# A bias that enters a PSUM bank by a three-row matmul instead of a ScalarE copy, and sums moved between two products (graph convolution, one Trainium2 core)

## The chip, the core and the metric

The kernel runs on one core of one Trainium2 chip. Its engines each run their own list of instructions in order and wait for each other by semaphores: PE (TensorE, matrix products into PSUM; its weight loads are shown apart as PEld), DVE (VectorE), ACT (ScalarE), POOL (GpSimd, which here issues scatters) and SP (SyncE, which issues the other transfers). The metric is the device time of one execution in microseconds.

## The reference

A graph layer over 12,500 nodes with 128 features and 412,500 edges, sorted by destination:

```python
h = jnp.maximum(_layernorm(x, axis=-1), 0.0)        # 12500 x 128
hh = h @ W_in2f
Wij = ssp(f_ij @ W_f1 + b_f1) @ W_f2 + b_f2         # per edge; f_ij is 412500 x 20, ssp = softplus - log 2
Wij = Wij * rcut_ij[:, None]
x_ij = hh[idx_j] * Wij                              # idx_j = dst
agg = segment_sum(x_ij, idx_i)                      # idx_i = src
out = x + ssp(agg @ W_o1 + b_o1) @ W_o2 + b_o2
```

The change concerns `b_f2`, which is added to the second product of every edge.

## The kernel before

Edges are worked off in chunks of 512 (four tiles of 128), four chunks to a group. There are 836 chunks: 660 plain ones, and 176 of the groups listed in SORTED ("permuted" groups), whose edges are first brought into another order on the core (class Permute: prefix counts and products with one-hot matrices, in "ready", "product", "taken" and "moved" phases spread over the steps ahead). No scatter of a permuted chunk starts after 3750 us.

A chunk passes through these stages:

- `hidden`: z = f @ W_f1 for two chunks at once (PE); `hidden_exp` and `hidden_log` make the softplus r from it (ACT).
- `window` and `pick`: a one-hot matrix `at` selects the rows of h for each edge out of a narrow table, four products into a PSUM bank called picked (PE).
- `picked`: hg = picked times the edge's weight, four ACT instructions.
- `bias` and `value`: a PSUM bank v is filled with b_f2, by an ACT copy (for the first two chunks by a product with a row of ones), and r @ W_f2 is accumulated on it, four float32 products on PE that don't clear the bank.
- `message`: o = v * hg (DVE).
- `put`: one indirect DMA per tile writes o to slots in DRAM (POOL): four scatters in a plain chunk. In a permuted chunk only the first tile is scattered, and the other three go out by a static transfer of SP.
- `blocks`, `rank`, `rank_end`: each edge's slot is a running count per node block; PE accumulates counts in the bank free, DVE reads their maximum (top).

The edges are cut into six segments (SEGS). When a segment has been scattered, class Collect reads its slots back (`load`, SP, into m), compares (`compare`, DVE, into to) and sums them per node (`add`, PE, into the bank acc); `keep` adds a finished bank to agg (ACT for the first segment, DVE later). The first such sums run after 1300 us; those of the last segment follow after the loop.

Everything is put in order by hand: `step(k)` issues, for each engine, the pieces of several chunks. Before the change PE's order within a step is value of chunk k+1, picking of chunk k+2, products of the permuting, hidden, rank, and the sums of the step's slots. ACT's is exponent, copies of permuted data, hg of chunk k+1, copy of b_f2 for chunk k+2, logarithm. The banks of picked and v share one pool of three. PACE makes the first scatter of chunk k wait for the picking of chunk k+2.

The banks that the change touches are v (filled at L969, products at L976) and picked (L985); hg is L994 and L1121, the message L1005 and L1131, the scatters L1014 and L1137, the sums L1430, keep L1451 and L1453, the exponent L871, the logarithm L876, the copy out of z L1330.

Of the kernel before, what the change touches and what calls it, by code (L numbers as in the profile page):

```python
# [69 lines left out]
def gnn_kernel(  # L70
# [142 lines left out]
    def sbuf(name, shape, dtype=F32):  # L213
        return const.tile(shape, dtype, name=name)

    def spread(t, n):
        return t[:, None, :].to_broadcast([t.shape[0], n, P])
# [20 lines left out]
    bf1, bo1 = (sbuf(n, [P, 1]) for n in ("bf1", "bo1"))  # L238
    bf2, bo2 = (sbuf(n, [P, P]) for n in ("bf2", "bo2"))
    nbo1 = sbuf("nbo1", [P, 1])  # L240
    spare = sbuf("spare", [P, 1])
    prow = sbuf("prow", [WP, 1])
    ones = sbuf("ones", [P, 1])
# [162 lines left out]
    def clear_sums():  # L406

        nc.vector.memset(exps, 0.0)

    def permute_constants():  # L410

# [286 lines left out]
    with tc.tile_pool(name="edge", bufs=2) as edge, tc.tile_pool(  # L698
# [65 lines left out]
        class Group:  # L764
# [194 lines left out]

            def bias(self, c):  # L960


                v = psum.tile([P, QT, P], F32, name="v", bufs=3)
                if self.g * NCHUNK + c < 2:
                    nc.tensor.matmul(v.rearrange("p t f -> p (t f)"),
                                     ones[0:1, :].to_broadcast([1, P]), spread(bf2[0:1, :], QT),
                                     start=True, stop=False, skip_group_check=True)
                else:
                    nc.scalar.activation(v, spread(bf2, QT), AF.Copy)  # L969
                return v  # L970

            def value(self, c, v):

                r = self.pair[c // 2 * 2][:, c % 2, :]
                for i in range(QT):
                    done = nc.tensor.matmul(v[:, i, :], r[:, i * P:(i + 1) * P], wf2,  # L976
                                     start=False, stop=True, skip_group_check=True)
                behind_of["value", place_of[self.g, c]] = done.ins.name
                return v
# [479 lines left out]
        def of(k):  # L1459
            return groups[steps[k][0]], steps[k][1]  # L1460

        hgs, ats, vs, bs = {}, {}, {}, {}

        compared = []
        owed = []
# [47 lines left out]
        def step(k, units=(), aside=()):  # L1513

            def has(j):
                return 0 <= j < NCH

            group(steps[max(0, min(k + LG, NCH - 1))][0])  # L1520
            part("rows", min(k + LW, 2 * k + 3, NEXT if k < NEXT - 3 else NCH), rows)
            for out_, in_ in statics:
                nc.sync.dma_start(out_, in_)
            statics.clear()
            if not aside:
                sorting(k, "taken")
            part("exp", min(k + LZ - 1, made["hidden"]), pairs(hidden_exp))
            if has(k):
                g, c = of(k)
                g.message(c, vs.pop(k), hgs.pop(k))  # L1530
            sorting(k, "moved")
            if aside:
                sorting(k, "taken")
            for m in aside:
                next(m, None)
            if k == place_of[permuted[-1], 0]:
                all_moved()
            if has(k + 1):
                g, c = of(k + 1)
                hgs[k + 1] = g.picked(c, ps.pop(k + 1))  # L1540
                vs[k + 1] = g.value(c, bs.pop(k + 1))
            if has(k + 2):
                g, c = of(k + 2)
                ps[k + 2] = psum.tile([P, QT, P], F32, name="picked", tag="v", bufs=3)
                g.pick(c, ats.pop(k + 2), ps[k + 2])
                if k + 2 > 0:
                    bs[k + 2] = g.bias(c)
            part("blocks", min(k + LR + 1, 2 * k + 3), blocks)
            for c, u in units:
                c.compare(u)  # L1550
                compared.append((c, u))
            if has(k):
                g, c = of(k)
                g.put(c)
            sorting(k, "product")
            part("hidden", k + LZ, pairs(hidden))
            for m in aside:
                next(m, None)
            part("log", min(k + LZ - 2, made["exp"]), pairs(hidden_log))
            for r in tops:  # L1560
                for _ in r:
                    pass
            tops.clear()
            upto = max(made["rank"], min(k + LR, 2 * k + 3))
            ready = [ranks(j) for j in range(made["rank"] + 1, upto + 1)]
            made["rank"] = upto
            for r in ready[:-1]:
                for _ in r:
                    pass
            for r in ready[-1:]:  # L1570
                next(r, None)
                tops.append(r)
            for c in owed:
                c.keep()
            owed.clear()
            part("window", k + 3, window)
            for c, u in units:
                c.load(u + AHEAD)
            for c, u in compared:
                c.add(u)  # L1580
            compared.clear()
            sorting(k, "ready")

        zeros = {}
# [143 lines left out]
        with tc.manual_schedule():  # L1728
# [22 lines left out]
            next(h[0])  # L1751
            part("rows", 1, rows)
            clear_sums()
            bs[0] = groups[0].bias(0)
            group(1)
            aside = side()
            prepares = permute_constants()
# [173 lines left out]
```

## Time and profile before

| | |
|---|---|
| median of 3 runs | 4806.63 us (4789.95 to 4812.86) |
| profiled execution | 4812.01 us, span 4809.8 us |
| mean granted PE clock | 0.855 |
| ACT copies of b_f2 (L969) | 834, 605 ns each |
| value products (L976) | 6688 records (two for each float32 product), 304 ns mean |
| scatters (L1014, L1137) | 2640 and 176, 964 and 962 ns |
| sums of slots (L1430) | 8492 records, 305 ns mean |

A row of the grouped views has the line, engine, operation, tiles written and read, count; then the busy time in us, the mean ns of one, the idle time of the engine just ahead of these instructions and what ended most of it. Matmuls overlap, so the busy time of a group is less than count times mean. In a timeline row stand start, duration, engine, line, operation, and in brackets the idle time before it with what ended it. "issue" means that the profile shows nothing that was waited for, "remote" that the one who ended the wait isn't told.

### The profile page before, as it was taken

The page shows a single profiled execution, that of the slowest core. Times are in us where ns is not written, and L with a number is a line of the kernel's source. Part 1 is how long each engine was busy: PE and PEld are TensorE (multiplying, and loading weights), DVE is VectorE, ACT ScalarE, POOL GpSimd, SP SyncE. Part 2 cuts the span into 40 slices and gives each one's busy share as a digit, 9 for nine tenths or more (in the row PEclk, how much of TensorE's full clock was granted, in tenths as well). Part 3 has the DMA queues.
Part 4 walks back from the last instruction along what each step waited for, and adds up shares of the span by engine and source line. Part 5 has one row for each costly group of instructions (what it writes and reads, how often), then busy time and mean ns, then how long its engine had stood idle before and what let it go on. Part 6 is the DMA issues. An engine that isn't in the chain of part 4 may idle for free. (4 is left out here: it accounts for less than half of the span.)

```text
span 4809.8 us, 81802 instructions
## 1 busy us (share of the span) xinstructions
PE 3657.9 (76%) x24283; PEld 2818.2 (59%) x24356; DVE 3165.3 (66%) x8788; ACT 2541.9 (53%) x5816; POOL 2716.4 (56%) x2834
## 2 busy tenths in 40 slices
PE   6666676666667777777877778888777878888878
PEld 4444444444446556665656666666666666676767
DVE  6667666655556666666666666767756666666667
ACT  4566566655655555555555555555544444444434
POOL 4655556555655555555555555555556666666650
PEclk8777778777778898888888888889989999889999
DMA  5676555544546655556655556667667787666666
GB/s 155 188 254 209 146 166 171 170 135 122 140 138 197 169 167 163 150 163 207 198 143 147 148 161 170 174 195 215 189 179 204 203 233 213 183 184 189 186 176 193
DMA packets 745252, 853.19 MB, mean 177 GB/s; under 512 B 288269, under 2 KB 546077, under 8 KB 744801
## 3 DMA queue, kind: packets, MB, share of 16 engines
q1 hardware_dynamic: 654256, 661.57, 50.8%
q0 software_dynamic: 90112, 186.17, 11.6%
q8 instruction: 198, 3.24, 0.3%
q14 instruction: 254, 2.07, 0.1%
q10 hardware_dynamic: 432, 0.13, 0.0%
HBM read 427.59 MB, written 402.53 MB: 173 GB/s over the span
## 5 line engine op out<-in xcount | busy, mean ns | idle before, releaser
L1014 POOL DMA_INDIRECT slots<-o,slot x2640 | 2544.3, 964 | 1625.3 <-issue 650.6
L1430 PE MATMUL acc<-to,m 128*128 128x128 f32 (+1 forms) x8492 | 1241.2, 305 | 194.3 <-issue 116.1
L1430 PEld LDWEIGHTS acc<-to,m 128*128 128x128 f32 (+1 forms) x8492 | 1186.4, 218 | 329.5 <-issue 190.0
L976 PE MATMUL v<-wf,r 128*128 128x128 f32 x6688 | 1041.7, 304 | 128.5 <-issue 76.4
L976 PEld LDWEIGHTS v<-wf,r 128*128 128x128 f32 x6688 | 961.4, 218 | 229.9 <-issue 145.2
L871 ACT ACTIVATE r<-z,bf 128x1024 f32<-128x1024 f32 x418 | 464.6, 1111 | 1085.7 <-remote 387.7
L994 ACT ACTIVATE hg<-picked,rcut 128x128 f32<-128x128 f32 x2640 | 748.2, 369 | 510.5 <-PE acc L1430 181.6
L1005 DVE TENSOR_TENSOR o<-v,hg 128x512 f32<-128x512 f32 x660 | 453.2, 687 | 672.9 <-remote 221.4
L1414 DVE TENSOR_TENSOR to<-count_ps,m 128x640 f32<-128x640 f16 (+6 forms) x988 | 678.0, 721 | 102.4 <-ACT scalars L1343 38.3
L969 ACT ACTIVATE v<-bf 128x512 f32<-128x512 f32 x834 | 504.9, 605 | 114.4 <-DVE o L1005 40.2
L911 DVE TENSOR_REDUCE top<-free 128x4 f32<-128x392 f32 x660 | 368.0, 558 | 213.0 <-remote 87.0
L985 PE MATMUL picked<-near,at 96*128 96x128 bf16 x2640 | 283.6, 234 | 264.9 <-issue 84.2
L876 ACT ACTIVATE r<-r,half 128x1024 f32<-128x1024 f32 x418 | 476.2, 1139 | 0.0
L863 PE MATMUL z<-f,wf 20*128 20x512 f32 x1320 | 430.7, 728 | 9.2 <-issue 5.1
L937 PE MATMUL free<-inb,rest_of 128*128 128x392 f16 x704 | 258.2, 367 | 227.4 <-DVE top L911 119.7
L985 PEld LDWEIGHTS <-at 96*128 96x128 bf16 x2640 | 223.2, 106 | 312.4 <-issue 260.8
L880 DVE TENSOR_TENSOR inb<-count_ps,blk 128x392 f16<-128x392 f16 x660 | 365.3, 554 | 1.5 <-PE acc_p L1264 1.5
L1137 POOL DMA_INDIRECT slots<-o,slot_p x176 | 169.3, 962 | 325.6 <-PE picked L985 150.5
L1121 ACT ACTIVATE hg<-picked,scalars 128x128 f32<-128x128 f32 x704 | 199.5, 370 | 129.9 <-remote 67.5
L906 PE MATMUL free<-inb,after 128*128 128x392 f16 x660 | 244.0, 370 | 18.6 <-DVE used L943 9.5
L1330 ACT ACTIVATE xo<-z 128x1024 bf16<-128x1024 f32 x88 | 90.0, 1023 | 272.5 <-PE z L1325 122.7
L956 DVE TENSOR_SCALAR at<-rel,prow 96x512 bf16<-96x512 bf16 x660 | 233.1, 353 | 0.0
(228 smaller groups left out, 3113.4 us busy)
## 6 DMA issues: line engine op xcount, KB each, us to landing
m<-slots SPq DMA_DIRECT2D x360, 322.5 KB
m<-slots SPq DMA_DIRECT2D x222, 387.0 KB
rel<-rel_d SPq DMA_DIRECT2D x165, 384.0 KB
slots<-zero SPq DMA_DIRECT2D x98, 516.0 KB
slots<-o,slot POOLq DMA_INDIRECT x2640
fix<-o SPq DMA_DIRECT2D x176, 193.5 KB
f<-in_f_n SPq DMA_DIRECT2D x416, 80.0 KB
m<-slots SPq DMA_DIRECT2D x90, 258.0 KB
```

The costliest lines, as they stand in the source:

```text
L863: nc.tensor.matmul(z[:, k, :], wf1[rows, :], self.f[rows, :], start=True, stop=True)
L871: nc.scalar.activation(r, z, AF.Exp, bias=bf1, accum_out=exps[:, i:i + 1])
L876: nc.scalar.activation(r, r, AF.Ln, bias=half, scale=0.5)
L911: nc.vector.tensor_reduce(self.top[:, c * QT:(c + 1) * QT], free_v, axis=mybir.AxisListType.X, op=ALU.max)
L969: nc.scalar.activation(v, spread(bf2, QT), AF.Copy)
L976: done = nc.tensor.matmul(v[:, i, :], r[:, i * P:(i + 1) * P], wf2, start=False, stop=True, skip_group_check=True)
L985: done = nc.tensor.matmul(ps[:, i, :], at[:, i * P:(i + 1) * P], near, start=i == 0, stop=i == QT - 1, skip_group_check=True)
L994: nc.scalar.activation(hg[:, i, :], ps[:, i, :], AF.Copy, scale=self.rcut[:, j:j + 1])
L1005: nc.vector.tensor_mul(o[:, :, :P], v, hg)
L1014: put = nc.gpsimd.indirect_dma_start(out=views[next(turns) % VIEWS], out_offset=bass.IndirectOffsetOnAxis(ap=self.slot[:, j:j + 1], axis=0 ...
L1414: nc.vector.tensor_tensor(to[:p, a:e, :], count_ps[:p, None, :].to_broadcast([p, e - a, P]), self.m[u][:p, a:e, P:].to_broadcast([p, e - a ...
L1430: nc.tensor.matmul(self.acc[b // self.size][:, i, :], m[:p, j, :P], to[:p, j, :], start=t == 0, stop=t == self.seg.read(b) - 1)
```

## The change

b_f2 is split once, at the start, into three bfloat16 rows whose sum is the float32 row (six DVE instructions in `clear_sums`). For all chunks but the first two, v is then started by one product of three rows of ones with these three rows, in place of the ACT copy. The bank is taken just ahead of the value products and no longer a step earlier. Four things move in `step(k)`: hg and value of chunk k+1 go to the head of the step, ahead of the exponent and of the message; the slots that were compared in the step before are summed between value and picking (they were summed at the end of their own step); keep, unmoved, now follows in the same step as the sums; and the logarithm goes ahead of the side work that prepares the tables.

```diff
+    ones3, bf2_parts = (sbuf(n, [P, P], BF16) for n in ("ones3", "bf2_parts"))
...
     def clear_sums():
         nc.vector.memset(exps, 0.0)
+        nc.vector.memset(ones3, 1.0)
+        w = ln.tile([P, P], F32, name="w_left", bufs=1)
+        def high(a):
+            return a.bitcast(BF16).rearrange("p (f h) -> p f h", h=2)[:, :, 1]
+        nc.vector.tensor_scalar(bf2_parts, high(bf2), ident[:, 0:1], None, op0=ALU.mult)
+        nc.vector.tensor_sub(w, bf2, high(bf2))
+        nc.vector.scalar_tensor_tensor(bf2_parts, high(w), ident[:, 1:2], bf2_parts,
+                                       op0=ALU.mult, op1=ALU.add)
+        nc.vector.tensor_sub(w, w, high(w))
+        nc.vector.scalar_tensor_tensor(bf2_parts, high(w), ident[:, 2:3], bf2_parts,
+                                       op0=ALU.mult, op1=ALU.add)
...
             def bias(self, c):
...
                 else:
-                    nc.scalar.activation(v, spread(bf2, QT), AF.Copy)
+                    nc.tensor.matmul(v.rearrange("p t f -> p (t f)"), ones3[:3, :],
+                                     spread(bf2_parts[:3, :], QT),
+                                     start=True, stop=False, skip_group_check=True)
                 return v
-            def value(self, c, v):
+            def value(self, c):
+                v = self.bias(c)
...
         def step(k, units=(), aside=()):
...
             statics.clear()
+            if has(k + 1):
+                g, c = of(k + 1)
+                hgs[k + 1] = g.picked(c, ps.pop(k + 1))
+                vs[k + 1] = g.value(c)
             if not aside:
                 sorting(k, "taken")
             part("exp", min(k + LZ - 1, made["hidden"]), pairs(hidden_exp))
...
-            if has(k + 1):
-                g, c = of(k + 1)
-                hgs[k + 1] = g.picked(c, ps.pop(k + 1))
-                vs[k + 1] = g.value(c, bs.pop(k + 1))
+            for c, u in compared:
+                c.add(u)
+            compared.clear()
             if has(k + 2):
...
                 g.pick(c, ats.pop(k + 2), ps[k + 2])
-                if k + 2 > 0:
-                    bs[k + 2] = g.bias(c)
...
             part("hidden", k + LZ, pairs(hidden))
+            part("log", min(k + LZ - 2, made["exp"]), pairs(hidden_log))
             for m in aside:
                 next(m, None)
-            part("log", min(k + LZ - 2, made["exp"]), pairs(hidden_log))
...
                 c.load(u + AHEAD)
-            for c, u in compared:
-                c.add(u)
-            compared.clear()
             sorting(k, "ready")
...
-            bs[0] = groups[0].bias(0)
```

The instructions of SP and POOL keep their order, and DVE's too but for the six at the start. On PE, around the value products of chunk 720 (a plain one; wf_63 is W_f2, after is a constant of the ranking, `[waits ...]` names the engines and DMA queues that an instruction waits for), there stood:

```order
L906 LDWEIGHTS after
L906 MATMUL free<-inb,after 128x392
L1430 MATMUL acc<-to,m 128x128 [waits DMAHW7_49]
L1430 MATMUL acc<-to,m 128x128 x4
L1430 MATMUL acc<-to,m 128x128 [waits DMAHW2_49]
L1430 MATMUL acc<-to,m 128x128 [waits DMAHW3_49]
L1430 MATMUL acc<-to,m 128x128 x3
L976 MATMUL v<-wf_63,r 128x128 [waits PE_49,Activation_49]
L976 MATMUL v<-wf_63,r 128x128 x3
L985 LDWEIGHTS at [waits DVE_49]
L985 MATMUL picked<-near,at 128x128 [waits DVE_49]
```

The sums stood ahead of the value products; these waited for ACT (the copy of b_f2), and the picking for DVE (the message, whose bank it takes). In the same place now:

```order
L982 LDWEIGHTS ones_71
L982 MATMUL v<-bf_parts,ones_71 128x512
L992 MATMUL v<-wf_63,r 128x128 [waits Activation_49]
L992 MATMUL v<-wf_63,r 128x128 x3
L1446 MATMUL acc<-to,m 128x128 [waits DMAHW7_49]
L1446 MATMUL acc<-to,m 128x128 x4
L1446 MATMUL acc<-to,m 128x128 [waits DMAHW2_49]
L1446 MATMUL acc<-to,m 128x128 [waits DMAHW3_49]
L1446 MATMUL acc<-to,m 128x128 x3
L1001 LDWEIGHTS at [waits DVE_49]
L1001 MATMUL picked<-near,at 128x128 [waits Activation_49]
```

The bias product and the value products stand ahead of the sums, and the picking's first row waits for ACT (hg of the chunk before). On ACT, in a stretch with permuted chunks (scalars are a permuted chunk's weights, xo takes its permuted features out of z), before:

```order
L876 ACTIVATE r<-r,half 128x1024
L871 ACTIVATE r,exps<-z,bf_66 128x1024
L1121 ACTIVATE hg<-picked,scalars 128x128 x4
L969 ACTIVATE v<-bf_68 128x512
L1330 ACTIVATE xo<-z 128x1024
L1121 ACTIVATE hg<-picked,scalars 128x128 x4
L969 ACTIVATE v<-bf_68 128x512
L876 ACTIVATE r<-r,half 128x1024
```

and now:

```order
L890 ACTIVATE r<-r,half 128x1024
L1137 ACTIVATE hg<-picked,scalars 128x128 x4
L885 ACTIVATE r,exps<-z,bf_66 128x1024
L1137 ACTIVATE hg<-picked,scalars 128x128 x4
L1346 ACTIVATE xo<-z 128x1024
L890 ACTIVATE r<-r,half 128x1024
```

hg has moved ahead of the exponent and of the copy out of z, and the copies of b_f2 are gone.

More of the change, by code (lines that the diff above doesn't have):

```diff
@@ L1460, in of @@
             return groups[steps[k][0]], steps[k][1]
-        hgs, ats, vs, bs = {}, {}, {}, {}
+        hgs, ats, vs = {}, {}, {}
         compared = []
```

## The prediction

> **What bounds the kernel now.** I read the page first (shares by engine, costliest groups), then busy time by stage, then the waits of POOL, then two pieces of the timeline.
>
> ```profile
> span 4809.8 us, 81802 instructions
> ...
> PE 3657.9 (76%) x24283; PEld 2818.2 (59%) x24356; DVE 3165.3 (66%) x8788; ACT 2541.9 (53%) x5816; POOL 2716.4 (56%) x2834
> ...
> L1014 POOL DMA_INDIRECT slots<-o,slot x2640 | 2544.3, 964 | 1625.3 <-issue 650.6
> ...
> L969 ACT ACTIVATE v<-bf 128x512 f32<-128x512 f32 x834 | 504.9, 605 | 114.4 <-DVE o L1005 40.2
> ```
>
> No engine is full. PE is the busiest at 76%, and the work to be removed is 505 us of ScalarE, which has room. POOL's share of 56% misleads: its 2640 scatters show 964 ns each, but most follow each other after another 0.3 us that is not counted as busy (650.6 us over the 2080 waits put down to issue). So a chunk's four scatters hold POOL for about 4 x 1.27 = 5.1 us. By stage:
>
> ```profile
> 3750.00:4640.00 890.00, 732.33 (x5275) 619.17 (x5275) 571.34 (x1233) 405.00 (x938) 552.68 (x577) 0.91 0.70 197
> 2500.00:3650.00 1150.00, 918.50 (x6396) 738.13 (x6419) 778.76 (x2086) 600.65 (x1382) 642.32 (x668) 0.88 0.63 175
> ...
> 130.00:1300.00 1170.00, 785.84 (x4520) 520.87 (x4539) 753.19 (x2496) 704.41 (x1633) 682.85 (x704) 0.78 0.59 170
> ```
>
> The columns are the stretch, its length, busy time and count of PE, PEld, DVE, ACT and POOL, the granted clock, DMA share and GB/s. In the last stretch there are only plain chunks: 577 scatters are 144.25 steps, 890/144.25 = 6.17 us a step, of which PE is busy 732.33/144.25 = 5.08 us. What sets 6.17? The timeline there:
>
> ```profile
> 4261.27 0.96 POOL L1014 DMA_INDIRECT slots<-o,slot  x1 [1.35 <-PE picked L985]
> ...
> 4262.53 0.96 POOL L1014 DMA_INDIRECT slots<-o,slot  x1 [0.30 <-issue]
> ...
> 4263.80 0.96 POOL L1014 DMA_INDIRECT slots<-o,slot  x1 [0.30 <-issue]
> ...
> 4264.99 0.39 PE L985 MATMUL picked<-near,at 96*128 96x128 bf16 x4
> ...
> 4265.06 0.96 POOL L1014 DMA_INDIRECT slots<-o,slot  x1 [0.30 <-issue]
> ...
> 4267.14 1.14 ACT L994 ACTIVATE hg<-picked,rcut 128x128 f32<-128x128 f32 x4 [2.63 <-PE acc L1430]
> 4267.15 0.69 DVE L1005 TENSOR_TENSOR o<-v,hg 128x512 f32<-128x512 f32 x1 [2.22 <-PE acc L1430]
> 4267.38 0.96 POOL L1014 DMA_INDIRECT slots<-o,slot  x1 [1.36 <-PE acc L1430]
> ```
>
> From first scatter to first scatter is 6.11 us: four scatters, then a pause of 1.36. The scatter at 4267.38 is ordered behind the picking that PE had finished at 4265.38, two microseconds earlier; ScalarE and VectorE, which wait for PE too, go on in the same moment, about 1.1 us after POOL's last scatter ended (4266.02). So here PE's results reach the others only when POOL's row of scatters is over. The chain is row of scatters, pause, row of scatters; PE has over 2 us of slack in it. POOL's waits tell how often the pause is missing:
>
> ```profile
> POOL slots L1014 <- issue: 133.7, 436, 0.6
> ...
> L1014 POOL DMA_INDIRECT slots<-o,slot x1913 | 1845.8, 965 | 1179.3 <-issue 480.0 <-PE picked L985 176.8 <-remote 167.0
> L1137 POOL DMA_INDIRECT slots<-o,slot_p x176 | 169.3, 962 | 325.6 <-PE picked L985 150.5 <-remote 26.4 <-PE z L1325 16.2
> ...
> POOL slots L1014 <- issue: 480.0, 1523, 5.6
> ```
>
> The first row is of 3750 to 4640 us: 436 short gaps, and three in each of 144 chunks make 433, so practically every chunk begins with a pause. The other three are of 130 to 3650 us: 1523 short gaps for 1913 scatters, of which 1435 lie inside chunks. In about 88 of 478 plain chunks POOL ran on into the next chunk without a pause, each time saving some 1.05 us (1.36 less 0.31). In that stage there are also 176 chunks of permuted groups with a single scatter (with the 660 plain chunks of 2640 scatters, 836 steps in all). If plain chunks take 6.11 us, less the 88 savings, they fill 2829 of the 3520 us, which leaves 3.9 us for each permuted one. There POOL is not the limit:
>
> ```profile
> 2645.89 0.96 POOL L1137 DMA_INDIRECT slots<-o,slot_p  x1 [4.06 <-PE picked L985]
> ...
> 2645.45 1.89 PE L1325 MATMUL z<-hot,slab 128*128 128x512 bf16 x7
> ...
> 2647.51 1.50 PE L1430 MATMUL acc<-to,m 128*128 128x128 f32 x12
> ...
> 2648.85 1.06 PE L976 MATMUL v<-wf,r 128*128 128x128 f32 x8
> ...
> 2649.74 0.39 PE L985 MATMUL picked<-near,at 96*128 96x128 bf16 x4
> ...
> 2650.41 0.96 POOL L1014 DMA_INDIRECT slots<-o,slot  x1 [3.56 <-PE picked L985]
> ```
>
> PE works almost without a gap from scatter to scatter, and the next scatter starts 0.28 us after the picking ends. So PE sets the time of permuted chunks, POOL with its pause that of plain ones.
>
> **The change, part by part.** The sum is made against the profiled execution, 4812.01 us (span 4809.8), which stands 5 us above the median of 4806.63.
>
> ```profile
> L1063 PE MATMUL z<-xo,w1s 96*128 96x512 bf16 x528 | 153.3, 434 | 0.0
> ...
> L1325 PE MATMUL z<-hot,slab 128*128 128x512 bf16 x394 | 117.1, 419 | 18.5 <-issue 11.5 <-ACT r L871 4.7
> ```
>
> *The bias product on PE.* 834 new products of 3 rows, 512 columns, bfloat16. None of three rows is in the trace; the nearest have the same columns and type with 96 and 128 rows: 153.3/528 = 0.290 and 117.1/394 = 0.297 us of PE each when they follow one another. The mean of one, 0.434, is the upper end. As the columns stream either way I take 0.29 and no gain from fewer rows; the weight load runs beside other matmuls. In all 834 x 0.29 = 242 us of PE (362 at the upper end). The page "TensorE: Matmul & The Clock Gate" of the Trainium skill (section Back-to-back issue gap) gives 215.7 ns warm and 426.7 cold for 512 columns; at this trace's mean clock of 0.855 that is an estimate of 0.25, or 208 us in place of 242. The rows lie a little above it.
>
> In plain chunks this costs nothing: PE goes from 5.08 to 5.37 us of a step of 6.17 in the fullest stretch, under cover of the scatters and their pause. If that cover went, it would be 660 x 0.29 = 191 us. In the 176 permuted chunks it stands in PE's own order ahead of the picking: 176 x 0.29 = +51 us.
>
> *No copy on ScalarE.* It frees 505 us of an engine that is 53% busy. What counts is only where PE waited for it:
>
> ```profile
> PE picked L985 <- ACT hg L994: 74.3, 35, 8.4
> PE picked L985 <- ACT hg L1121: 60.4, 22, 9.2
> PE acc L1430 <- DVE agg L1453: 40.0, 27, 7.5
> PE v L976 <- ACT v L969: 29.4, 16, 8.1
> ...
> PE acc L1430 <- ACT agg L1451: 18.5, 8, 4.5
> ```
>
> The wait of the value products for the copy, 29.4 us, goes wholly. With permuted chunks a fifth of all steps (176 of 836), 6 us of it is on the path; the weight loads show the same stalls, which doubles nothing.
>
> *picked and value moved to the step's head.* On ScalarE hg now stands ahead of the exponent and of the copy out of z where there is one, so the pickings that waited 134.7 us for hg wait less; a fifth, 28 us, is on the path. Against that, the picking's first row now waits for ScalarE (hg of the step before) where it often waited for VectorE's message. Bounds: from a loss of about one hg, 1.14 us, in each permuted chunk (201 us) to a gain of those 28. I take 0.8 of the 28, 22 us, since in the piece above the value and sum products lie between and cover an hg.
>
> *Slots summed between value and picking.* The sums and the value products swap places on PE; POOL's scatter still waits for the same set of products, so nothing is gained for the picking. What is queued behind a sum that waits for its rows from DMA or for its bank (40.0 + 18.5 us) is now the picking, and before it was value and picking. keep gets a step's value products as extra cover: a fifth of 58.5, 12 us, at most; I take half, 6. The sums free their m buffers after the value products, 1.35 us later (1.06 + 0.29), and SP's next loads of m wait so much longer; they are ordered three units ahead, so I count nothing, with 0 to 20 us as bounds.
>
> *The logarithm ahead of the side work.* Same engine, same inputs, no wait added: 0. *Six VectorE instructions at the start*, by the memset's row at most 0.41 us each, 2.5 us together:
>
> ```profile
> 16.91 0.41 DVE L408 MEMSET exps<- 128x418 f32 x1 [0.44 <-ACT r L871]
> ...
> 25.85 0.69 DVE L1005 TENSOR_TENSOR o<-v,hg 128x512 f32<-128x512 f32 x1 [5.73 <-ACT hg L994]
> ```
>
> They come where VectorE then idles 5.73 us, so 0, at most 2.5.
>
> Sum: +51 - 6 - 22 - 6 = +17 us on 4812, or 4824 from the median. The prologue and the end, some 300 us, keep their times. Against this small loss stands an unknown in the plain chunks, the number of times that POOL runs on (88 now): hg's earlier place makes PE's next picking earlier, and 20 more run-ons would give 21 us back. I take the two as cancelling: 4805 us.
>
> **The rivals.**
>
> *Faster: the waits removed are on the path in plain chunks too.* For it speaks that in 88 chunks POOL did run on, so an earlier picking is worth 1.05 us there, and that the waits listed above sum to 222.6 us. If half of that comes back, 111 us, and the product is hidden, it ends near 4700. Against it: in the late timeline the picking was finished 2 us before it was noticed. It decides once more than about 40 further chunks run on.
>
> *Slower: run-ons are lost.* The picking of the next chunk can no longer be issued until ScalarE has seen the previous one and made hg (1.14 us), with 0.29 of bias and up to 1.5 of sums ahead of it; if it comes too late in the row of scatters, POOL pauses. All 88 lost are +92 us, with the 51 of the permuted chunks +143; with half of both lost, 4880. It decides once some 25 run-ons are gone. Against it: hg has been put first on ScalarE.
>
> *Slower by far: PE is the bound everywhere.* Then the whole product shows, 4812 + 242 = 5050. The granted clock below 1 and PE's 76% speak for it, the 5.08 of 6.17 us against it. The page "Perfetto Trace Analysis" of the Trainium skill (section Identifying the Most-Contended Engine) says to relieve the engine with the highest occupancy first; this change does the reverse, and by that rule the kernel loses. The stage table is why I don't follow it.
>
> **How the numbers follow.** No change that shows, 0.43, at 4805. Faster by the earlier pickings, 0.32, around 4700 to 4780. Slower by lost run-ons, 0.21, around 4835 to 4890; PE the bound, 0.04. Within 0.5%, 24 us, a measurement of this kernel can hardly tell a change from none (its runs spread from 4789.95 to 4812.86), so: faster 0.32, same 0.43, slower 0.25. The range goes from the faster rival's 4700 to the slower one's 4890 and leaves out some 0.15. The likeliest case's own range is 4783 to 4830.
>
> **What would show it.** Right: in the last stage still 6.1 us a step with a pause near 1.36; PE busy up by 200 to 260 us; the bias product near 0.29 us; no wait of PE for v from ScalarE; permuted chunks near 3.9 us. Wrong towards faster: clearly more than 1523 short gaps before scatters up to 3650 us, or a pause below 1.3. Wrong towards slower: fewer short gaps, pickings that end just before their scatter in plain chunks, or PE waiting longer for hg than 134.7 us.

## The result: 0.8% slower, and the profile after

The changed kernel takes 4833.94 us (median of 8 runs, 4812.43 to 4854.28) where the kernel before takes 4798.99 on the same chip (8 runs, 4788.10 to 4812.86): 35 us more by the medians; the ratio of the two is put at 1.008, 95% interval 1.0061 to 1.0100, which would be 38 us. The forecast was 4805, no change that shows; the time is inside the range of 4700 to 4890, and outside the 4783 to 4830 given for the likeliest case. The profiled execution took 4854.28 us (span 4852.6), the longest of its eight and 42 us above the profiled one of before.

The page after, shares by engine and the groups that answer to those of before (line numbers have moved: L1014 is L1030, L1137 is L1153, and the copy L969 is now the product L982):

```profile
span 4852.6 us, 83109 instructions
...
PE 4037.1 (83%) x25190; PEld 2854.0 (59%) x25190; DVE 3167.5 (65%) x8794; ACT 2071.8 (43%) x4982; POOL 2717.0 (56%) x2834
...
L1030 POOL DMA_INDIRECT slots<-o,slot x2640 | 2544.2, 964 | 1628.7 <-issue 651.9
...
L1153 POOL DMA_INDIRECT slots<-o,slot_p x176 | 170.0, 966 | 362.1 <-PE picked L1001 122.1
...
L982 PE MATMUL v<-bf_parts,ones 3*128 3x512 bf16 x834 | 360.3, 432 | 8.5 <-issue 5.7
```

ScalarE lost 470 us of work and PE gained 379. Of these the new products are 360.3/834 = 0.432 us each, the upper end that the prediction had given (0.434) and not the 0.29 that it took. By stage (the columns as in the prediction):

```profile
3750.00:4640.00 890.00, 780.66 (x5450) 614.29 (x5449) 578.89 (x1257) 321.22 (x798) 557.29 (x581) 0.92 0.71 200
...
2500.00:3650.00 1150.00, 986.79 (x6618) 728.16 (x6619) 779.30 (x2108) 487.03 (x1173) 629.43 (x656) 0.89 0.61 172
```

The last stage, plain chunks alone, did 581 scatters in the 890 us where it had done 577: 890/145.25 = 6.13 us a step, with PE busy 780.66/145.25 = 5.37 us of it, the figure forecast. In the stage ahead of it, from 2500 to 3650 us, a quarter of the steps are permuted. It did 656 scatters where it had done 668; as 54 of them are of permuted chunks (52 before), that is 204.5 steps in place of 206. So the loss is to be looked for where permuted chunks are. A timeline of the last stage shows why the plain ones don't mind:

```profile
4264.11 0.96 POOL L1030 DMA_INDIRECT slots<-o,slot  x1 [0.30 <-issue]
...
4266.01 1.14 ACT L1010 ACTIVATE hg<-picked,rcut 128x128 f32<-128x128 f32 x4 [3.75 <-PE acc L1446]
...
4266.25 0.96 POOL L1030 DMA_INDIRECT slots<-o,slot  x1 [1.18 <-PE acc L1446]
...
4267.20 0.37 PE L982 MATMUL v<-bf_parts,ones 3*128 3x512 bf16 x1
...
4267.50 1.16 PE L992 MATMUL v<-wf,r 128*128 128x128 f32 x8
...
4272.27 0.96 POOL L1030 DMA_INDIRECT slots<-o,slot  x1 [1.27 <-remote]
```

The pause of POOL is still there (1.18 and 1.27 us), ScalarE still starts some 0.9 us after POOL's last scatter (which ended at 4265.07), and the product lies inside the row of scatters. It took 0.30 us from its start to the value product behind it (4267.20 to 4267.50); over all 834 the median of that distance is 0.31. The 0.432 of the group has the tail that overlaps the next product.

For an account of the whole, take the start of each chunk's first scatter and sum the 835 intervals by the kinds of the two chunks (permuted chunks stand in pairs, N N N N P P N N N N):

| intervals | before, us | after, us | difference |
|---|---|---|---|
| plain to plain, 571 | 3473 | 3445 | -28 |
| plain to permuted, 88 | 519 | 539 | +20 |
| permuted to permuted, 88 | 312 | 328 | +16 |
| permuted to plain, 88 | 326 | 358 | +32 |

The 264 intervals that touch a permuted chunk lost 68 us, the others gained 28. These are sums of one execution each, and the one after is the slowest of its eight, so they show where the time went better than how much it was. The next piece shows two such intervals, from the scatter at 2646.74 to that at 2650.06 and on to 2654.72:

```profile
2646.22 0.59 PE L982 MATMUL v<-bf_parts,ones 3*128 3x512 bf16 x1
...
2646.74 0.96 POOL L1153 DMA_INDIRECT slots<-o,slot_p  x1 [2.20 <-PE count_ps L1280]
...
2647.28 2.08 PE L992 MATMUL v<-wf,r 128*128 128x128 f32 x8
...
2649.15 0.63 PE L1001 MATMUL picked<-near,at 96*128 96x128 bf16 x4
...
2649.71 0.60 PE L982 MATMUL v<-bf_parts,ones 3*128 3x512 bf16 x1
...
2650.06 0.96 POOL L1153 DMA_INDIRECT slots<-o,slot_p  x1 [2.37 <-PE picked L1001]
...
2650.24 2.08 PE L992 MATMUL v<-wf,r 128*128 128x128 f32 x8
...
2654.05 0.39 PE L1001 MATMUL picked<-near,at 96*128 96x128 bf16 x4
...
2654.72 0.96 POOL L1030 DMA_INDIRECT slots<-o,slot  x1 [3.71 <-PE count_ps L1297]
```

POOL has one scatter and then waits for PE. PE's granted clock is 0.50 here (2645 to 2651 us): the product takes 0.53 us to the value product behind it (2649.71 to 2650.24), where it took 0.30 in the piece of the last stage, at 1.00. Over all intervals that begin with a permuted chunk, the mean clock is 0.81 as it was before, so the clock isn't what the change moved. Whose are the two products L982 here? The scatter of chunk k waits for the picking of chunk k+2, and ahead of that picking PE does the value of chunk k+1. With the pair at k = P1 and P2, the scatter of P2 waits for the picking of P2+2, behind the value of P2+1; the next scatter waits for the picking of P2+3, behind the value of P2+2. Both are plain chunks, two places behind a permuted one. This reading came only with the third experiment.

What PE waited for, in the whole run:

```profile
PE free L951 <- DVE top L925: 132.3, 56, 8.9
...
PE z L877 <- ACT xo L1346: 41.0, 14, 8.5
PE picked L1001 <- ACT hg L1010: 38.4, 18, 6.3
...
PE picked L1001 <- ACT hg L1137: 20.9, 9, 6.1
```

The waits for hg fell from 134.7 to 59.3 us, and none for v from ScalarE is left. But the hidden products now wait 41.0 us for the copy out of z (xo), ahead of which hg was put, where it had been 4.0, and the wait for the ranking's maximum (top) is 132.3 in place of 119.7. VectorE waits longer for the loads of m:

```profile
DVE to L1430 <- DMA m<-slots: 82.9, 61, 5.8
...
DVE to L1430 <- DMA m<-fix: 29.9, 36, 2.8
```

These were 15.1 and 5.9 us before. Of the 113 us, 94 lie between 3750 and 4640 us, where the steps became no longer.

### The profile page after: what moved, and what is told of

It is laid out like the page before. It is cut to its first block, busy times and chain, and to the rows that moved or that the text cites. A ratio compares the mean times of both kernels' runs of the same rounds, so it can differ in the third digit from the quotient of the medians.

```text
span 4852.6 us, 83109 instructions
## 1 busy us (share of the span) xinstructions
PE 4037.1 (83%) x25190; PEld 2854.0 (59%) x25190; DVE 3167.5 (65%) x8794; ACT 2071.8 (43%) x4982; POOL 2717.0 (56%) x2834
## 5 line engine op out<-in xcount | busy, mean ns | idle before, releaser
L1030 POOL DMA_INDIRECT slots<-o,slot x2640 | 2544.2, 964 | 1628.7 <-issue 651.9
L1446 PE MATMUL acc<-to,m 128*128 128x128 f32 (+1 forms) x8492 | 1185.4, 297 | 137.0 <-issue 81.9
L1446 PEld LDWEIGHTS acc<-to,m 128*128 128x128 f32 (+1 forms) x8492 | 1130.4, 213 | 156.2 <-issue 97.3
L992 PE MATMUL v<-wf,r 128*128 128x128 f32 x6688 | 1163.5, 325 | 33.8 <-issue 31.7
L992 PEld LDWEIGHTS v<-wf,r 128*128 128x128 f32 x6688 | 975.1, 223 | 336.8 <-issue 321.2
L1430 DVE TENSOR_TENSOR to<-count_ps,m 128x640 f32<-128x640 f16 (+6 forms) x988 | 689.0, 720 | 305.2 <-DMA m<-slots 82.9
L877 PE MATMUL z<-f,wf 20*128 20x512 f32 x1320 | 440.8, 740 | 51.3 <-ACT xo L1346 41.0
L951 PE MATMUL free<-inb,rest_of 128*128 128x392 f16 x704 | 260.1, 369 | 218.9 <-DVE top L925 132.3
L1137 ACT ACTIVATE hg<-picked,scalars 128x128 f32<-128x128 f32 x704 | 201.0, 373 | 413.6 <-remote 135.4
L1153 POOL DMA_INDIRECT slots<-o,slot_p x176 | 170.0, 966 | 362.1 <-PE picked L1001 122.1
L982 PE MATMUL v<-bf_parts,ones 3*128 3x512 bf16 x834 | 360.3, 432 | 8.5 <-issue 5.7
L982 PEld LDWEIGHTS <-ones 3*128 3x128 bf16 x834 | 76.9, 92 | 298.8 <-issue 296.2
```

What stands on the lines that cost most here:

```text
L877: nc.tensor.matmul(z[:, k, :], wf1[rows, :], self.f[rows, :], start=True, stop=True)
L982: nc.tensor.matmul(v.rearrange("p t f -> p (t f)"), ones3[:3, :], spread(bf2_parts[:3, :], QT), start=True, stop=False, skip_group_check=True)
L1030: put = nc.gpsimd.indirect_dma_start(out=views[next(turns) % VIEWS], out_offset=bass.IndirectOffsetOnAxis(ap=self.slot[:, j:j + 1], axis=0 ...
L1430: nc.vector.tensor_tensor(to[:p, a:e, :], count_ps[:p, None, :].to_broadcast([p, e - a, P]), self.m[u][:p, a:e, P:].to_broadcast([p, e - a ...
L1446: nc.tensor.matmul(self.acc[b // self.size][:, i, :], m[:p, j, :P], to[:p, j, :], start=t == 0, stop=t == self.seg.read(b) - 1)
```

## The experiments

Theory 1 said that the product costs time in the intervals set by PE. Theory 2 said that the new order costs it, by later loads of m and by hidden products that wait for xo. Each kernel was compared with the kernel before on its own chip, and the chips were not alike: for some of the runs the kernel before took 3817.48 or 3825.00 us, for the others 4796.9 to 4841.02. The expectations call the former the fast chip; the section on hardware shows it. In microseconds a difference of two ratios is given as that difference times 4800. All ratios (to the kernel before, with the 95% interval; a kernel with again or third behind its name is the same kernel on another occasion):

| kernel | products | chip as in the forecast | the fast chip |
|---|---|---|---|
| the change | 834 | 1.008 [1.0061, 1.0100] | 1.0244 [1.0220, 1.0269] |
| order_copy | 0 | 0.9981 [0.9959, 1.0004] | 1.0061 [1.0048, 1.0074] |
| product_old | 834, old order | 1.0163 [1.0132, 1.0194], 1.0165 [1.0138, 1.0192] | not run |
| plain_only | 658 | 1.0099 [1.0060, 1.0138] | not run |
| sums_end | 834 | 1.0128 [1.0093, 1.0163], 1.0130 [1.0099, 1.0161] | not run |
| copy_behind | 658 | 0.9994 [0.9975, 1.0014] | 1.0200 [1.0177, 1.0223], 1.0238 [1.0210, 1.0267] |
| product_behind | 176 | 1.0070 [1.0041, 1.0100] | 1.0052 [1.0034, 1.0070], 1.0069 [1.0057, 1.0082] |
| twice_behind | 834 + 176 | 1.0144 [1.0113, 1.0174] | 1.0238 [1.0217, 1.0259] |
| twice_others | 834 + 658 | 1.0102 [1.0068, 1.0135] | 1.0387 [1.0360, 1.0413] |

**order_copy: the new order alone.** The copy of b_f2 goes back to ScalarE, a step ahead; all else is the changed kernel.

```diff
-                    nc.tensor.matmul(v.rearrange("p t f -> p (t f)"), ones3[:3, :],
-                                     spread(bf2_parts[:3, :], QT),
-                                     start=True, stop=False, skip_group_check=True)
+                    nc.scalar.activation(v, spread(bf2, QT), AF.Copy)
...
                 g.pick(c, ats.pop(k + 2), ps[k + 2])
+                if k + 2 > 0:
+                    bs[k + 2] = g.bias(c)
```

> The order of the changed kernel, but the ScalarE copy of b_f2 instead of the product (a step ahead, after the picking, where it stood before). Theory 1, the product in the permuted chunks: in the profiled pair the steps that begin or end with a permuted chunk grew by 68 us and those from plain to plain shrank by 28, so the product costs about 0.39 us in each of 176 permuted chunks and the new order gains about 28. Then this kernel ends near 4799 - 30 = 4770 us (4755 to 4785), below the kernel before. Theory 2, the new order: later loads of m (VectorE waits for them 113 us in place of 21), hidden products that wait for the copy out of z (41 us in place of 4); the product is hidden. Then it stays near 4830 (4820 to 4845).

0.9981, that is -9 us with an interval from -20 to +2: theory 2 falls, the order by itself isn't what costs. VectorE's waits for m are there as with the change (102.0 us in place of 21.0), and cost nothing that shows. The gain of 30 us that theory 1 had read from the plain intervals is not there either: they sum to 3473 us, as before. PE's waits for hg did fall, without the change of product:

```profile
PE picked L998 <- ACT hg L1134: 39.0, 14, 6.9
PE picked L998 <- ACT hg L1007: 37.5, 22, 6.9
...
PE v L989 <- ACT v L982: 28.8, 23, 4.9
PE acc_p L1349 <- ACT xo L1343: 28.8, 5, 6.4
...
PE z L877 <- ACT xo L1343: 21.9, 17, 6.0
```

The waits for hg are 76.5 us in place of 134.7, and the run is at most 20 us shorter. Those for xo are 50.7 us; before they were 10.9 (6.9 and 4.0). So of the 58 us that one wait lost, the next gained 40.

**product_old: the product alone**, in the order of before, just ahead of the value products. The cut is against the kernel before; what prepares the three rows is as in the change.

```diff
-            def value(self, c, v):
+            def value(self, c):
+                v = self.bias(c)
...
-                    nc.scalar.activation(v, spread(bf2, QT), AF.Copy)
+                    nc.tensor.matmul(v.rearrange("p t f -> p (t f)"), ones3[:3, :],
+                                     spread(bf2_parts[:3, :], QT),
+                                     start=True, stop=False, skip_group_check=True)
```

> The order of the kernel before, but the three-row product instead of the ScalarE copy, just ahead of the value products. Theory 1, the product in the permuted chunks: 4799 + 68 = 4867 us (4845 to 4880), with the growth in steps that touch a permuted chunk alone. Theory 2, the new order is what costs: 4799, no change within 10 us. The slope theory that PE bounds everything would give 4799 + 834 x 0.31 = 5058.

1.0163, 78 us. The plain intervals kept their 3473 us, those that touch a permuted chunk went from 1157 to 1256. The product costs, and in these two traces (of two chips) only there.

**plain_only: the product taken out of the permuted chunks.**

```diff
-                    nc.tensor.matmul(v.rearrange("p t f -> p (t f)"), ones3[:3, :],
...
+                    if self.g in permutes:
+                        nc.scalar.activation(v, spread(bf2, QT), AF.Copy)
+                    else:
+                        nc.tensor.matmul(v.rearrange("p t f -> p (t f)"), ones3[:3, :],
...
+                if g.g in permutes:
+                    bs[k + 2] = g.bias(c)
```

> The changed kernel, but the 176 permuted chunks get b_f2 by the ScalarE copy again (a step ahead); the 658 plain ones keep the product. Theory 1: the product costs only in permuted chunks, so 4834 - 68 = 4766 us (4750 to 4785), faster than the kernel before. Theory 2, the new order: 4834 less at most 5, since order and product of the plain chunks are unchanged. Should the product cost in the plain chunks that stand between permuted ones, it ends between, at 4785 to 4820.

1.0099: nothing came back, and theory 1 in its first form missed by some 80 us. The intervals that touch a permuted chunk still sum to 1228 us, although no permuted chunk has a product any more. That led to the reading above: these intervals hold the products of the chunks two places on.

**sums_end: the sums at the end of their own step again.**

```diff
-            for c, u in compared:
-                c.add(u)
-            compared.clear()
             if has(k + 2):
...
                 c.load(u + AHEAD)
+            for c, u in compared:
+                c.add(u)
+            compared.clear()
             sorting(k, "ready")
```

> The changed kernel, but the sums of slots stand at the end of their own step again, so that the buffers of m come free as early as before. Theory 1, the product in the permuted chunks: no change, 4834 within 15 us, though VectorE's waits for m fall from 113 us back to about 20 (94 of the 113 lie in the last stage, whose steps did not grow). Theory 2, later loads of m: 4800 to 4810, the loss goes with the waits.

1.0128, slower than the change, against both theories. VectorE's waits for m did fall, to 17.0 us, and the loss didn't go with them. With the product on PE, sums between value and picking are worth some 0.5% (24 us). Why isn't settled: with the copy, the whole new order and the old one are within 0.4% of each other (order_copy).

**copy_behind and product_behind: which products cost.** In copy_behind the 176 chunks two places behind a permuted one get the ScalarE copy and the 658 others the product; product_behind is the reverse.

```diff
+        def after_p(k):
+            return k >= 2 and steps[k - 2][0] in permutes
...
-                    nc.tensor.matmul(v.rearrange("p t f -> p (t f)"), ones3[:3, :],
...
+                    if after_p(place_of[self.g, c]):
+                        nc.scalar.activation(v, spread(bf2, QT), AF.Copy)
+                    else:
+                        nc.tensor.matmul(v.rearrange("p t f -> p (t f)"), ones3[:3, :],
...
+                if after_p(k + 2):
+                    bs[k + 2] = g.bias(c)
```

> The changed kernel, but the 176 chunks that stand two places behind a permuted chunk get b_f2 by the ScalarE copy; all others keep the product. Theory 1, new form: the scatter of a permuted chunk k waits for the picking of chunk k+2, and in PE's order the value products of chunk k+1 stand just ahead of that; the two intervals that PE sets thus hold the products of the two plain chunks behind the pair, not the permuted chunks' own (so leaving the product out of those own chunks brought nothing: 1.0099). Then the loss goes here: ratio 0.990 to 1.000 to the kernel before. Rival, any plain chunk's product costs in the mixed stage (658 plain chunks, 0.07 us each): 482 of 658 plain chunks still have it, so the ratio stays above 1.005. Rival, mixing copy and product costs by itself: 1.008 or more.

> The new order, with the product only in the 176 chunks two places behind a permuted chunk, and the ScalarE copy in all others. Theory 1, new form: all of the loss with a fifth of the products: ratio 1.006 to 1.013 to the kernel before. Rival, every plain chunk's product costs: 0.998 + 0.0102 x 176/658 = 1.001.

**twice_behind and twice_others: a second, idle product**, in those 176 or in the 658 others.

```diff
-                    nc.tensor.matmul(v.rearrange("p t f -> p (t f)"), ones3[:3, :],
-                                     spread(bf2_parts[:3, :], QT),
+                    for _ in range(2 if after_p(place_of[self.g, c]) else 1):
+                        nc.tensor.matmul(v.rearrange("p t f -> p (t f)"), ones3[:3, :],
+                                         spread(bf2_parts[:3, :], QT),
...
```

> The changed kernel, with the product issued twice (same operands, the second overwrites the first) in the 176 chunks two places behind a permuted chunk. Theory 1, new form: 176 x 0.31 to 0.49 us = 55 to 86 us more than the changed kernel: ratio 1.019 to 1.026. Rival, the product costs nearly nothing there: 1.008 to 1.012.

> The changed kernel, with the product issued twice in the 658 other chunks. Theory 1, new form: POOL sets those intervals, so no change to the changed kernel: ratio 1.005 to 1.012. Rival, every plain chunk's product costs 0.07 us or more: 1.008 + 482 x 0.07/4840 = 1.015 at least; PE the bound: 1.008 + 658 x 0.31/4840 = 1.050.

These four ran on the fast chip, and there the new theory failed: 1.0200 and 1.0052 where it asked for below 1 and above 1.006, 1.0387 for the doubled product in the 658 others. twice_behind at 1.0238 lay inside its range by luck, since the change itself turned out to lie at 1.0244 there. The four can't be held against the 1.008 of the other chip, so the change itself was run there, with three of the others:

> The changed kernel itself, beside the next three, because the four runs before this one fell on a chip on which the kernel before takes 3817 us and POOL's rows of scatters run on without a pause (1883 short gaps, 110 us of pauses in all, against 1261 us of pauses in the first profile). If this chip is like that one (call it the fast chip): there 176, 658 and 1492 products cost 20, 77 and 148 us, about 0.11 us each wherever they stand, so 834 of them cost 85 to 100: ratio 1.020 to 1.027. If it is like the first one (4800 to 4840 us before): 1.008 as before (1.005 to 1.012).

> The new order with the ScalarE copy for every chunk. Theory 1: the order gives and takes nothing, 0.995 to 1.003 on either chip. Rival: the new order costs on the fast chip (product_behind's 1.0052 would then be the order, not the products): 1.004 or more.

> ScalarE copy in the 176 chunks two places behind a permuted one, product in the 658 others. On a chip like the first: theory 1 in its new form (the loss is the products in the two intervals that PE sets) 0.990 to 1.000; the rivals (any plain chunk's product costs, or mixing costs) above 1.005. On the fast chip again 1.02.

> Product only in the 176 chunks two places behind a permuted one, ScalarE copy in the 658 others. On a chip like the first: theory 1 in its new form 1.006 to 1.013, the rival (every plain chunk's product costs) 1.001. On the fast chip again 1.005.

There the change is at 1.0244, its order alone 1.0061 (theory 1 had said at most 1.003). So on this chip the order costs about 0.6%, the product on top of it another 1.8%. On a chip like the first, the same question again:

> ScalarE copy in the 176 chunks two places behind a permuted one, product in the 658 others. If this is a chip like the first (POOL pauses between rows, before at 4800 to 4840 us): theory 1 in its new form (the loss there is the products in the two intervals that PE sets) 0.990 to 1.000, the rivals above 1.005. If it is the fast chip: 1.02 to 1.024 as twice before.

> Product only in the 176 chunks two places behind a permuted one. On a chip like the first: theory 1 in its new form 1.006 to 1.013, the rival (every plain chunk's product costs alike) 1.001. On the fast chip 1.005 to 1.007.

> The order of the kernel before with the product for all but two chunks. On a chip like the first 1.016 again. On the fast chip order and product came to 1.0061 and another 0.018: if the new order is what costs 0.6% there, this kernel ends at 1.018; if the old order suits the product worse, as on the first chip, above 1.024.

> The changed kernel with the sums of slots at the end of their own step again. On a chip like the first 1.013 again. On the fast chip, where VectorE waits 183 us for loads of m in the changed kernel: 1.018 if these waits are the 0.6% of the new order, 1.024 or more if they are hidden.

copy_behind 0.9994: 658 products, next to order_copy, cost (0.9994 - 0.9981) x 4800 = 6 us, within their interval of 15. product_behind 1.0070: 176 products cost 43 us next to order_copy (interval 25 to 60), of the 48 that all 834 cost. That mixing copy and product costs by itself falls with copy_behind too. One execution each: the intervals that touch a permuted chunk sum to 1171 us with the first and 1255 with the second (1157 before, 1225 with the change). The other two repeat their first results; what they were to tell of the fast chip stays open. The doubled products on a chip like the first:

> The changed kernel with the product issued twice in the 176 chunks two places behind a permuted one. On a chip like the first: the second product does nothing but take PE's time, so it shows what one product costs in the intervals that PE sets: 176 x 0.31 us (the median distance from its start to the value product behind it) is 55 us, ratio 1.019; at 0.49 (the mean of that distance from 130 to 3650 us) 86 us, 1.026. On the fast chip 1.024 again, next to nothing above the changed kernel.

> The changed kernel with the product issued twice in the 658 other chunks. On a chip like the first POOL sets those intervals with PE over half a microsecond short of them, so 1.005 to 1.012, no more than the changed kernel; if the cover gives out at the second product, up to 1.008 + 658 x 0.31/4840 = 1.050. On the fast chip 1.039 again.

twice_others 1.0102: the second product costs 11 us (interval -8 to 29) where 658 x 0.31 = 204 us were added to PE's work; nearly all of it is hidden. Its last stage has PE busy 804 of 890 us and still 579 scatters:

```profile
3750.00:4640.00 890.00, 804.23 (x5571) 609.96 (x5571) 576.26 (x1252) 320.10 (x794) 556.16 (x579) 0.93 0.70 199
```

twice_behind 1.0144 missed its 1.019 to 1.026: the second product costs 31 us (interval 13 to 48), 0.17 each. In its intervals 36 us more are spent at the permuted chunks than with the change, and 11 less from plain to plain.

The products two places behind stand in the intervals that begin with a permuted chunk: permuted to permuted and permuted to plain. On chips like the first, one execution each, the sums of these intervals go with those products. They are 638 us before, 633 with order_copy and 653 with copy_behind, which have none there; 677 (twice_others) to 729 (product_old) in the kernels that have one, with 686 for the change and 705 for plain_only; and 735 with twice_behind, which has two. Kernels with none and with one don't overlap; what a second adds is lost in the spread. PE's granted clock is part of that spread: in these intervals it is 0.81 in the traces of the three kernels with none, of the change and of twice_others, and 0.78 to 0.79 in all the others. At 0.81 the one product thus takes the sum from 633 to 653 us up to 677 to 686. Whether the lower clock makes the other kernels slower, or comes from how their PE waits, isn't shown.

## Why the prediction was wrong, point by point

*The product, 51 less 6 us: right in size in the new order, too small in the old.* Change less order_copy is (1.0080 - 0.9981) x 4800 = 48 us, interval 33 to 62, and it has both terms in it. In the order of before the product costs 78 us, interval 63 to 93 (product_old), where the prediction had 45. Each of the 176 products behind a permuted chunk costs 0.24 us in the new order (product_behind less order_copy, 43/176; 0.14 to 0.34), which agrees with the 0.29 taken. The two traces would say 0.41 ((1225 - 1153)/176) with 28 us back from plain to plain, but one is the slowest execution of its eight and the other the fastest of its twelve, on another chip.

*Plain chunks hide it: right*, shown by copy_behind, and by twice_others even for two products. Where the prediction spoke of products that stand "in PE's own order ahead of the picking", it counted the permuted chunks' own, and those aren't the ones that cost (plain_only): those of the chunks two places on are on the path (product_behind). That the count is 176 either way is luck; each pair of permuted chunks has two such chunks behind it.

*The step that failed: the credits of the new order, read off waits and added to the product's price as if neither depended on the other.* The prediction took -22 for hg, -6 for keep and -21 for 20 further run-ons, -49 in all, and let the last cancel what loss the sum had left. order_copy puts all of them to the test without the product: -9 us, from -20 to +2. The waits for hg did shorten, by 58 us, and those for xo grew by 40; "0.8 of the 28" was a share of a wait taken for a share of time. Next to the product the same order is worth more: 78 us with product_old, 38 with the change, so 40 (22 to 57), of which the place of the sums makes some 24 (sums_end). So the sum can be taken in two ways, and in both one of its terms is off by over 30 us: credits of 9 and a price of 48, or a price of 78 and credits of 40. Order and product by themselves add up to 78 - 9 = 69 us, together they are 38. The forecast, which had 45 - 49 = -4 us, has no term for this difference of 31 us, and how it comes about stays open. In the traces a lower granted clock goes with it (0.79 with product_old in the intervals that begin with a permuted chunk, 0.81 with the change).

*The run-ons.* From plain to plain, counted by the gap itself (under 0.45 us) and not by what it is put down to, they were 146 before and not 88. They went to 155 with the order alone, and those intervals kept their 3473 us. With the change they are 164, 18 more and so close to the 20 of the forecast, and those intervals are 28 us shorter; that they are so because permuted chunks come later is a guess that no run tests.

*The signs.* The steps of the last stage (6.13 us) and the wait for v came as said. PE's busy time rose by 379 us and not by 200 to 260. The signs named for wrong contradict each other: the median pause of the last stage fell from 1.34 to 1.28 us, named for faster, and the short gaps up to 3650 us went from 1523 to 1513, named for slower, while PE waited less for hg and not longer. An interval that begins with a permuted chunk took 3.62 us before, not the 3.9 of the prediction, and takes 3.90 now.

*Later loads of m, counted as nothing: right on this chip.* The waits came (113 us), 94 of them in the last stage, where the steps became no longer; with order_copy they came too (102 us) without a loss, and sums_end took them away without a gain. *Logarithm and start:* not tried one by one; order_copy holds them too. The first scatter starts at 33.6 us in place of 32.9.

*The rivals.* Faster fell with order_copy. Slower by lost run-ons had the sign right, not the cause: run-ons became more. PE the bound everywhere fell here by twice_others; the rule of the Trainium skill ("Perfetto Trace Analysis", Identifying the Most-Contended Engine) that the engine with the highest occupancy comes first warned rightly of the sign. That section tells to judge TensorE by the busy share of its weight loads, though; here that is 59%, below VectorE's 66%, so by it the rule need not name PE at all. If it does, more work on PE should go on costing, and in twice_others another 111 us of busy PE (4148.2 against 4037.1) cost nothing that can be told from none. On the fast chip, where PE is busy 3268.0 of 3847.4 us (85%) already with order_copy, a rule that names PE and the runs agree: there the change loses 2.4%.

No kernel tried is shown to be faster than the one before.

## What to carry to other kernels

A wait in the table is not time: before crediting an earlier result, ask what that engine would wait for next, and try the reordering by itself. When work is added to an engine that sets only some of the steps, find which items' work is issued ahead of the wait in those steps; with a pipeline that looks two items ahead it belongs to other items than the step's own name. And a cover made of another engine's pauses holds only where those pauses are: measure it on the chip that will run the kernel.

## What the runs showed of the hardware

The pause that covers the product isn't there on every chip. The change on the fast chip, page, POOL's waits and a timeline:

```profile
span 3904.4 us, 83109 instructions
...
PE 3587.2 (92%) x25190; PEld 2581.0 (66%) x25190; DVE 3154.3 (81%) x8794; ACT 2082.8 (53%) x4982; POOL 2725.7 (70%) x2834
```

```profile
POOL slots L1030 <- issue: 143.9, 472, 0.3
POOL slots L1030 <- PE picked L1001: 21.5, 20, 5.8
```

```profile
3005.80 0.39 PE L1001 MATMUL picked<-near,at 96*128 96x128 bf16 x4
...
3006.22 1.14 ACT L1010 ACTIVATE hg<-picked,rcut 128x128 f32<-128x128 f32 x4 [2.02 <-PE picked L1001]
...
3006.38 0.96 POOL L1030 DMA_INDIRECT slots<-o,slot  x1 [0.30 <-issue]
...
3007.61 0.39 PE L982 MATMUL v<-bf_parts,ones 3*128 3x512 bf16 x1
3007.64 0.95 POOL L1030 DMA_INDIRECT slots<-o,slot  x1 [0.30 <-DVE inb L894]
```

The waits are those of 2900 to 3700 us. A scatter lasts 0.96 us as on the other chip, but ScalarE sees the picking's end (3006.19) at once, in the middle of a row, and POOL goes from row to row with 0.30 us between: in 536 of the 571 intervals from plain to plain, against 164 on the first chip. Plain intervals last 5.18 us in place of 6.03 (2960/571 and 3445/571). One piece of a timeline could mislead, so take all of ScalarE's starts that ended a wait of 0.4 us or more for PE. On the fast chip 610 of 783 lie inside a row of scatters, and the 660 rows of 4.8 us fill 81% of the span; on the first chip 150 of 646 do, where the rows fill 65%. So on the first chip most of PE's results, though not all as the prediction's piece might suggest, were taken up only between rows.

What made them late on the first chip goes with the chip or its state and not with the program; what it is, no run here shows. PE's granted clock differs too (0.943 on the fast chip, 0.848 on the first, in the profiled executions of the change), while the median float32 product of L992 takes 275 ns on both; whether the lower clock is a cause of the pauses or comes from them isn't tested.

Where the product costs turns round with it. On the fast chip, the 658 products outside the 176 cost 1.4 to 1.8% (copy_behind less order_copy, 53 to 68 us), a second one in the same chunks 1.4% (twice_others less the change, 55 us), and the 176 cost nothing that can be told from none (product_behind 1.0069 against order_copy 1.0061; twice_behind 1.0238 against the change 1.0244). That PE, at 92%, then works against a POOL without pauses fits the first two; why the 176 are free there, and whether the later loads of m make the order's 0.6% (VectorE waits 183 us for them with the change, 174 with order_copy), stays open.
